# Four changes of order in a four-layer graph kernel: x loads, a batch norm, LSTM sums and differences, start-up

## The chip, the cores and the metric

One core of a Trainium2 chip runs the whole program. The metric is the device time of one execution in microseconds (us); lower is better. Everything is fp32.

## The reference

The input is x with the shape (128, 64, 256): 128 graphs of 64 nodes with 256 features, and one 64 x 64 adjacency `adj`. Four layers follow one another, each as `x = x + layer(relu(layernorm(x)), adj)`:

```python
# layer 0: two graph convolutions, then four LSTMs over windows of the nodes
h = relu(einsum('ts,bsh->bth', adj, h @ Wg0 + bg0))
h = relu(einsum('ts,bsh->bth', adj, h @ Wg1 + bg1))
for p in range(1, 5):                      # window length p
    wins = h[:, :nw*p].reshape(B*nw, p, H)
    h[:, last node of each window] = lstm_last(Wih[p-1], Whh[p-1], ..., wins)
# layer 1: masked attention, 4 heads
q, k, v = split(h @ W);  out = softmax(q k^T / 8 + mask(adj)) v
# layer 2: x @ W1^T -> batch norm -> relu -> @ W2^T -> batch norm, on A_hat h
# layer 3: three graph convolutions with adj*adj, widths 512, 1024, 256
```

The two batch norms of layer 2 take mean and variance over all 8192 tokens, so nothing of layer 3 can start before the last token of layer 2.

## The kernel before, in words

The 8192 tokens are cut into 16 blocks of 512 (`NG = 16`; a block holds 8 graphs as a tile of 128 partitions x 4 x 256). Each layer runs over the blocks. x of a block is read from HBM into a tile `xs[g]` that stays on the chip to the end. Many matrix products are done as seven products of half-size blocks instead of eight (`seven`, `sevens`); these need a few sums of one operand's blocks (`sums`, lines 206 to 209) and differences of the other's (`differences`, lines 198 to 202), four element-wise instructions each.

The order of the work on each engine is fixed when the program is built. A planner walks through the instructions as the code issues them and places each on its engine when, by its own estimate, its inputs and its buffer are ready; an instruction that comes later in the code can so be put ahead of one that comes earlier. `tc.issue_after(i)` orders the instructions of its block behind instruction `i` on the same engine, and adds no other wait. `tc.keep_in_program_order` is used for the batch norm's instructions (`normalize`). Engines run what they are given in that order. The queues that matter here are those of TensorE (PE), VectorE (DVE), ScalarE (ACT), GpSimd (POOL), and SyncE (SP), which issues nearly all transfers.

The places that the change touches:

- **Start-up.** `keep_busy(n)` (line 308) issues n matmuls on a tile of ones that do nothing but keep TensorE at work. `by_batch` (line 297) turns the two halves of `arow`, the adjacency, into `pt`; fillers stand ahead of and between the halves. `adj2` is the copy of `pt` (line 314). `ln_scale` computes a layer norm's factors: statistics on DVE (lines 92 to 95), a power on POOL (line 96), and `nmr` on DVE (line 98). Its argument `between` gives an instruction behind which `nmr` is ordered. `ln_apply` (line 111) then makes h on ACT, and `mix` (line 144) multiplies it by the adjacency on PE. rb0 is a bias row, scaled in line 424.
- **Layer 0, convolutions.** A loop over blocks runs `first_mix(g)`, `second_weights(g - 2)`, `second_mix`, `first_weights`. On DVE each iteration has the statistics, copies out of PSUM (lines 157 and 409; `copied_of[g]` is that of line 409), and the bias additions of lines 453 and 474; POOL applies the relu of line 454; PE runs the matmuls of lines 144, 445 and 469.
- **LSTM.** `first_blocks` makes the sums of the weights of an LSTM's first step. For the first LSTM all four are ordered behind `middle_copied`, the copy of iteration 8. `first_steps` makes the differences of the windows; those of the first pair of units stand in a buffer of the pool `keep` and have no order given. The tiles of `lw` ("w", five buffers) hold the weights and these sums, taken in order; `load_w` (line 275) fills them.
- **Layer 1, attention.** In iteration g, `values` makes v in two parts k = 0 and 1 (PE line 810), copies it to the single buffer `vt` (ACT line 815) and moves it with four SP transfers (line 818) into `v`. Between the parts, `load_x` (line 58) asks for the x of block g + 5, and `queries_keys` (line 788) makes q and k. `features` (lines 265 and 198 to 202) makes hT and its differences for the next iteration. Then come `scores` (line 834), `softmax` (lines 852 to 854), `turn` (PE line 870, ACT line 873) and `attend` (line 883). `to_residual` (lines 245 to 256) adds layer 0's result to x of block g + 3.
- **Layer 3.** `bring(n, ahead)` carries out n returns of layer 2's result to x (`turn_back`, PE line 1116; `add_back`, DVE line 1124) and asks for `ahead` batch norms (`normalize`: ACT line 1104, DVE line 1106). In iteration 0, blocks 0 to 7 are brought before `second_weights` (PE line 1243, ACT lines 216 and 219); after it, `bring(0, 1)` normalizes block 8 and `bring(1, 1)` returns it and normalizes block 9. `third_weights` is PE line 1288, `first_weights` line 1207.

## Time and profile before

| | |
|---|---|
| median of 3 runs | 2482.23 us (2481.2 to 2482.25) |
| profiled execution | 2480.78 us, its span 2479.0 us |
| mean granted TensorE clock | 0.999 |
| idle of PE, by the waits: the longest single ones | 2.9 us (L1116), 2.3 us (L810), 1.1 us (L870) |
| DVE, ACT, POOL busy | 61%, 46%, 18% |
| transfers | 48.00 MB, 19 GB/s in the mean |
| x loads, 512 KB each | 27, median 6.1 us from issue to landing |
| v writes, 64 KB each | 128, median 2.1 us |

A line of a timeline reads: start (us from the span's start), time from start to end, engine, line of the kernel, operation, what it writes <- what it reads, shape, and how many instructions are merged; in brackets the idle time of the engine just before, and what ended it. SPq is SyncE's queue of transfers; its time is that of issuing. L1243 is line 1243. "LDWEIGHTS" and "MATMUL" come in pairs, and an fp32 matmul shows as two records.

### The profile page before, as it was taken

The numbers are of one execution on the slowest core, as the hardware profiler recorded it, in microseconds if no ns is written. First come the engines' busy times: TensorE is split into PE (matmuls) and PEld (weight loads), VectorE is DVE, ScalarE is ACT, GpSimd is POOL, SyncE is SP. The second block draws the span as 40 slices with busy tenths as digits, with TensorE's granted clock in tenths as the row PEclk, the third lists the DMA queues.
The fourth block names the chain that finished last, engine by engine and source line by source line (L and its number), as shares of the span: only waits on it lengthen the run. The fifth ranks groups of instructions, "written<-read, shape, count | busy, mean of one in ns | idle before, by whom it ended". The sixth has DMA issues, their size and how long they took to land.

```text
span 2479.0 us, 46321 instructions
## 1 busy us (share of the span) xinstructions
PE 2454.4 (99%) x19650; PEld 2073.3 (84%) x19650; DVE 1513.1 (61%) x2705; ACT 1145.5 (46%) x2032; POOL 439.6 (18%) x368
## 2 busy tenths in 40 slices
PE   9999999999999999999999999999999999999999
PEld 6678888889999998888888864447898898888888
DVE  6758866666566565566599986325556455454544
ACT  4557745444344443444456566744333323333332
POOL 4332211111111111111133331012011111101110
PEclk9999999999999999999999999999999999999999
DMA  3200000000000000000311110010000000000000
GB/s 115 104 2 1 1 18 1 1 1 34 1 1 1 1 1 1 1 13 1 115 40 36 40 32 2 1 59 1 10 10 18 10 10 13 16 10 10 18 10 18
DMA packets 48558, 48.00 MB, mean 19 GB/s; under 512 B 3680, under 2 KB 44768, under 8 KB 48352
## 3 DMA queue, kind: packets, MB, share of 16 engines
q1 hardware_dynamic: 47360, 44.23, 5.8%
q8 instruction: 154, 2.52, 0.4%
q10 hardware_dynamic: 992, 0.82, 0.1%
q14 instruction: 52, 0.43, 0.1%
HBM read 28.26 MB, written 8.39 MB: 15 GB/s over the span
## 4 chain that ended last, share of the span: by engine, by line
PE 84%; DVE 7%; ACT 2%; POOL 1%; issue 1%; DMA 0%; SPq 0%; DVEq 0%; POOLq 0%; ACTq 0%
PE ps L526 41%; PE ps L1243 16%; PE ps L1288 8%; PE ps L1076 4%; PE ps L755 4%; PE ps L144 3%; PE ps L1207 3%; PE ps L788 1%; PE ps L469 1%; PE ps L445 1%; ACT arena L219 1%; PE ps L810 1%; DVE st L92 1%; DVE e L853 1%; DVE mx L852 1%
## 5 line engine op out<-in xcount | busy, mean ns | idle before, releaser
L526 PE MATMUL ps<-diff,s 128*128 128x256 f32 (+1 forms) x1824 | 393.5, 371 | 0.9 <-DVE diff L643 0.9
L1243 PE MATMUL ps<-arena 128*128 128x256 f32 x1792 | 392.4, 380 | 0.0
L1243 PEld LDWEIGHTS ps<-arena 128*128 128x128 f32 x1792 | 337.9, 190 | 53.9 <-issue 9.2
L526 PEld LDWEIGHTS ps<-diff,s 128*128 128x128 f32 x1824 | 345.9, 190 | 33.8 <-issue 1.6
L540 ACT ACTIVATE gates<-gates,lbias 128x512 f32<-128x512 f32 (+5 forms) x426 | 244.2, 621 | 203.4 <-DVE gates L185 147.3
L180 POOL TENSOR_TENSOR gates<-p 128x512 f32<-128x512 f32 (+1 forms) x115 | 149.3, 1298 | 879.0 <-DVE p L177 828.1
L526 PE MATMUL ps<-h,w 128*128 128x256 f32 (+1 forms) x1028 | 241.0, 371 | 0.0
L526 PE MATMUL ps<-diff,w 128*128 128x256 f32 (+1 forms) x1040 | 238.7, 370 | 0.0
L526 PEld LDWEIGHTS ps<-diff,w 128*128 128x128 f32 x1040 | 197.4, 190 | 18.2
L526 PEld LDWEIGHTS ps<-h,w 128*128 128x128 f32 x1028 | 194.7, 190 | 19.0 <-issue 0.5
L540 ACT ACTIVATE gates<-ps,lbias 128x256 f32<-128x256 f32 (+3 forms) x213 | 91.6, 476 | 247.1 <-PE ps L526 246.9
L219 ACT ACTIVATE arena<-arena 128x512 f32<-128x512 f32 (+1 forms) x160 | 88.7, 582 | 193.1 <-POOL arena L180 101.2
L180 POOL TENSOR_TENSOR arena<-arena 128x512 f32<-128x512 f32 x64 | 73.2, 1144 | 532.3 <-DVE arena L177 532.3
L1288 PE MATMUL ps<-arena 128*128 128x128 f32 x1280 | 149.9, 276 | 0.0
L185 DVE TENSOR_TENSOR gates<-p,ps 128x512 f32<-128x512 f32 (+1 forms) x115 | 76.3, 664 | 120.0 <-PE ps L526 119.8
L1288 PEld LDWEIGHTS ps<-arena 128*128 128x128 f32 x1280 | 145.7, 192 | 1.1
L96 POOL TENSOR_TENSOR rstd<-rstd,mhalf 128x4 f32<-128x4 f32 (+1 forms) x66 | 66.1, 1002 | 423.0 <-DVE rstd L95 411.6
L185 DVE TENSOR_TENSOR arena<-arena,ps 128x512 f32<-128x512 f32 x64 | 39.7, 621 | 152.9 <-PE ps L1243 87.4
L526 PE MATMUL ps<-state,w 128*128 128x256 f32 (+1 forms) x512 | 116.1, 370 | 0.9 <-ACT p L173 0.8
L176 DVE TENSOR_TENSOR p<-p,ps 128x512 f32<-128x512 f32 (+1 forms) x131 | 86.6, 661 | 48.5 <-PE ps L526 48.4
L526 PE MATMUL ps<-state,s 128*128 128x256 f32 (+1 forms) x512 | 115.8, 369 | 0.0
L189 DVE TENSOR_TENSOR gates<-p,ps 128x512 f32<-128x512 f32 (+1 forms) x115 | 76.6, 666 | 63.9 <-PE ps L526 63.2
(206 smaller groups left out, 4070.2 us busy)
## 6 DMA issues: line engine op xcount, KB each, us to landing
x<-in_x SPq DMA_DIRECT2D x27, 512.0 KB, 6.1
v<-vt SPq DMA_DIRECT2D x128, 64.0 KB, 2.1
out<-x SPq DMA_DIRECT2D x15, 512.0 KB, 3.0
w<-in_wih SPq DMA_DIRECT2D x4, 1024.0 KB, 6.1
w<-in_whh SPq DMA_DIRECT2D x3, 1024.0 KB, 5.0
arena<-in_l3w SPq DMA_DIRECT2D x3, 1024.0 KB, 5.3
w<-in_wqkv SPq DMA_DIRECT2D x1, 768.0 KB, 4.5
x<-in_x SPq DMA_DIRECT2D x2, 256.0 KB, 3.0
```

What stands on the lines that cost most here:

```text
L144: last = nc.tensor.matmul(pss[b][half * 64 : half * 64 + 64, c, t, :], lhsT=src[rows, t, col : col + 64], rhs=a2[rows, :], start=True, sto ...
L176: nc.vector.tensor_tensor(p1, p1, ps[2], ALU.add)
L180: nc.gpsimd.tensor_tensor(out=out[1][1], in0=p1, in1=p5, op=ALU.add)
L185: nc.vector.tensor_tensor(out[0][1], p1, ps[1], ALU.add)
L189: last = nc.vector.tensor_tensor(to, p, q, ALU.add)
L219: nc.scalar.activation(o, o, func)
L526: nc.tensor.matmul(ps[:, r], lhsT=wc[:, j, :], rhs=bc, start=first and r == 0 and c == 0, stop=True, skip_group_check=True,)
L540: nc.scalar.activation(o, ps, func, bias=lbias[:, col : col + 1])
L755: nc.tensor.matmul(ps, lhsT=w1[:, c, m * P : (m + 1) * P], rhs=a[:, 2 + c, :], start=(c == 0), stop=(c == 1),)
L1076: nc.tensor.matmul(pss[m], lhsT=w2[c // 2][:, c % 2, m * P : (m + 1) * P], rhs=a[:, c, :], start=(c == 0), stop=(c == 3),)
L1243: nc.tensor.matmul(ps[:, r, :], lhsT=w[:, c, col : col + P], rhs=b[:, c, :], start=first and r == 0 and c == 0, stop=c == 1, skip_group_ch ...
L1288: nc.tensor.matmul(ps[:, t, :], lhsT=w[:, c, t * P : (t + 1) * P], rhs=b[:, c, :], start=first and t == 0 and c == 0, stop=c == 3, skip_gr ...
```

## The change

- Start-up: 6 fillers instead of 7 ahead of the first half of `pt`, 2 instead of 3 between the halves, 2 behind; the copy of `adj2` is placed ahead of the second half's `nmr` instead of the first's.
- LSTM: the four sums of the first LSTM's weights come one each behind `copied_of[5]` to `copied_of[8]`; the four differences of its first pair come one each behind `copied_of[10]` to `copied_of[13]`. They are written as loops over the four operations, with an order for each.
- Attention: `load_x` of block g + 5 is ordered behind the last of the four transfers of `values(..., (0,))`.
- Layer 3: in iteration 0, `bring(0, 1)` stands ahead of `second_weights` instead of behind it.

```diff
+    def each_behind(behind, i):
+        return tc.issue_after(behind[i].ins) if behind else nullcontext()
...
+    def differences(eng, b11, b12, b21, b22, t1, t2, t3, t4, negate=False, behind=None):
         t4a, t4b = (b21, t2) if negate else (t2, b21)
-        return eng.tensor_tensor(out=t4, in0=t4a, in1=t4b, op=ALU.subtract).ins
...
+        ops = ((t1, b12, b11), (t3, b22, b12), (t2, b22, t1), (t4, t4a, t4b))
+        for i, (t, p, q) in enumerate(ops):
+            with each_behind(behind, i):
+                last = eng.tensor_tensor(out=t, in0=p, in1=q, op=ALU.subtract)
+        return last.ins
...
-            keep_busy(7)
+            keep_busy(6)
             pt = bank((P, NODES))
-            by_batch(pt, arow, lambda b, last: keep_busy(3 - b, last))
+            by_batch(pt, arow, lambda b, last: keep_busy(2, last))
             lns = [
-                ln_scale(xs[0][:, 0:2], lambda: nc.vector.tensor_copy(adj2, pt), 2),
-                ln_scale(xs[0][:, 2:4], None, 2),
+                ln_scale(xs[0][:, 0:2], None, 2),
+                ln_scale(xs[0][:, 2:4], lambda: nc.vector.tensor_copy(adj2, pt), 2),
             ]
...
-                    differences(nc.vector, *x[0], *x[1], *ts, negate=True)
+                    differences(
+                        nc.vector, *x[0], *x[1], *ts, negate=True,
+                        behind=copied_of[10:14] if pool is keep else None,
+                    )
...
-            with tc.issue_after(middle_copied):
-                w0 = first_blocks(w_next[0], lw.tile([P, 2, 1024], F32, tag="w", name="s"))
+            w0 = first_blocks(
+                w_next[0], lw.tile([P, 2, 1024], F32, tag="w", name="s"), copied_of[5:9]
+            )
...
-            values(hT_all, v, (0,))
+            moved = values(hT_all, v, (0,))
             if g + NK + 1 < NG:
-                load_x(xs[g + NK + 1], g + NK + 1)
+                with tc.issue_after(moved):
+                    load_x(xs[g + NK + 1], g + NK + 1)
...
                 brought = ready
+                bring(0, 1)
...
                     for b, pss in later:
                         add_back(b, pss)
-                bring(0, 1)
             bring(1, 1)
```

`sums` is rewritten in the same way as `differences`, `first_blocks` hands `behind` on to it, and `values` returns its last transfer.

## The prediction

> **What bounds the kernel now.** I read the head of the page first: TensorE (PE) has almost no room.

> ```profile
> PE 2454.4 (99%) x19650; PEld 2073.3 (84%) x19650; DVE 1513.1 (61%) x2705; ACT 1145.5 (46%) x2032; POOL 439.6 (18%) x368
> ```

> With a span of 2479.0 us, PE is idle for 24.6 us in all. The change removes no matmul but two start-up fillers, so its gain can only come from that idle time, and each part has to be laid on a named gap. So the second view is the waits of PE (us in total, times, longest):

> ```profile
> PE ps L1116 <- ACT arena L1104: 3.2, 2, 2.9
> PE ps L810 <- ACT hT L265: 2.3, 1, 2.3
> PE ps L144 <- POOL h L454: 1.8, 4, 0.8
> PE ps L870 <- ACT e L854: 1.1, 1, 1.1
> ```

> The timeline puts the first at 1739.50 (layer 3), the second at 1239.81 and the fourth at 1246.37 (attention), and 1.2 of the third at 103.12 and 104.57 (layer 0). Third, the busy time by stretches of 3.4 us around 1739.5 (columns: length, busy PE, PEld, DVE, ACT, POOL, then the granted clock):

> ```profile
> 1736.60:1740.00 3.40, 0.50 (x5) 0.50 (x6) 3.40 (x4) 1.89 (x3) 0.00 (x0) 1.00 0.00 0
> 1740.00:1743.40 3.40, 3.40 (x72) 2.95 (x71) 3.25 (x6) 0.49 (x2) 0.00 (x0) 0.50 0.00 0
> ```

> The reader is to see that the gap is paid twice: PE idles, and then runs one stretch at half clock, busy but slow. From the first L1116 to the first L1288 takes 3.40 there and 2.06 one iteration later (1790.00 to 1792.06), and the next 48 L1288 take 5.84 against 5.62: 1.56 us more.

> [...]

> **Part E, the batch norm ahead of second weights.** bring(0, 1) issues two instructions for block 8: ACT L1104 (0.75) and DVE L1106 (0.54). No transfer goes with them. Now they come after second_weights in the code. ACT's timeline around it (start, duration, idle before it):

> ```profile
> 1710.16 0.58 ACT L154 COPY arena<-ps 128x512 f32<-128x512 f32 x1 [0.35 <-PE ps L144]
> 1714.20 0.58 ACT L173 COPY arena<-ps 128x512 f32<-128x512 f32 x1 [3.46 <-PE ps L1243]
> ...
> 1738.11 0.63 ACT L219 ACTIVATE arena<-arena 128x512 f32<-128x512 f32 x1 [1.89 <-DVE arena L189]
> 1738.64 1.50 ACT L1104 ACTIVATE arena<-arena,n2sh,n2sc 128x512 f32<-128x512 f32 x2
> ```

> L1104 stands behind the last L219 on ACT's queue, and PE's transposes L1116 at 1739.50 wait for it, though its data was ready long before. Moved, it falls in the idle 3.46 before 1714.20. That cover is 2.7 more than it needs; without it 0.75 would fall on the path. DVE's half moves from idle time at 1717.46 to just before the last differences, which PE's third product reads: L200 ends at 1714.42, with 0.54 more at 1714.96; the 112 L1243 are 14 products in 24.34, 1.74 each, so the third starts at 1712.22 + 3.48 = 1715.70. Hidden with 0.7 to spare. Then PE goes from L1243 into L1116 as at 1790.00, where no gap is. Late next could be the sums of third weights; L206 ends at 1737.47 and the second product would start near 1742.0. Gain: 2.94 of gap. The 1.56 of half clock goes too, but [...] not every run before needs to have paid it: I take half, 0.8 (0 to 1.56). **E: 3.7** (2.0 to 4.5).

> **Part D, loads of x.** In the timelines of SP and ACT:

> ```profile
> 1227.38 2.29 SPq L58 DMA_DIRECT2D x<-in_x  x4
> 1230.09 2.69 SPq L818 DMA_DIRECT2D v<-vt  x4
> ```

> ```profile
> 1238.68 0.58 ACT L815 COPY vt<-ps 128x512 f32<-128x512 f32 x1 [2.47 <-DMA v<-vt]
> 1239.16 1.08 ACT L265 COPY hT<-ps 128x512 f32<-128x512 f32 x2
> ```

> All twelve x loads (512 KB each) are issued between 1211.5 and 1232.8, because nothing holds them. The four writes of v behind them land near 1238.6, some 6 us after the last is issued, where the median is 2.1. vt has one buffer, so its next copy on ACT waits; hT, queued behind that, holds PE's L810 for 2.27; and because DVE's L198, scores and softmax follow hT, L870 at 1246.37 waits 1.05, where ordinary iterations lose 0.13. Moved, eleven loads (x5 to x15) each go behind the fourth v write of their iteration. Then v lands by 1232.8 + 2.1 = 1234.9; ACT ends L245 at 1236.2, L815 runs at once, and hT starts at 1236.7 instead of 1239.16. L810 can start when L834 ends (1237.53): the 2.27 goes. From hT's start to L870 takes 7.21 now (1239.16 to 1246.37), so L870 comes at 1243.9 instead of 1246.37. Gain 2.5; 3.2 if hT also gets as early as later on. The added wait: SP holds a load until the v writes are out. Behind it stand only the next writes of v, issued 6.4 us later; x of block g+5 is first added in iteration g+2, over 25 us on. **D: 2.5** (2.0 to 3.2).

> **Parts B and C, sums and differences of the LSTM.** DVE's timeline in layer 0:

> ```profile
> 91.28 0.69 DVE L206 TENSOR_TENSOR w<-w 128x512 f32<-128x512 f32 x1 [2.24 <-DMA w<-in_wih]
> ...
> 98.02 0.69 DVE L199 TENSOR_TENSOR diff<-h 128x512 f32<-128x512 f32 x1 [0.73 <-ACT h L477]
> ...
> 100.44 0.68 DVE L453 TENSOR_TENSOR h<-ps,rb 128x512 f32<-128x512 f32 x1
> ```

> In a quiet iteration L453 starts 2.03 after PE's L445; here the L445 began at 94.06, so it is over 4 us late, and POOL's L454 and PE's L144 follow it: gaps of 0.43 and 0.76, and 0.12 at 98.99. Between stand four differences (2.7), four sums for the second LSTM (2.7) and waits of 2.24 and 0.73. The change spreads the differences over iterations 10 to 13 and the first LSTM's sums over 5 to 8, one of 0.68 each. DVE idles 1.90 + 1.03 + 0.41 + 0.22 = 3.6 per quiet iteration of 9.47 (around 77 us), so each is hidden; without that cover, 0.68 each. What moves along: three weight loads of 1 MB start at 85.19, 0.7 after the first sum at 84.51, in the same pool; with that sum in iteration 5 they should start near 57. Then the second LSTM's sums and their DMA wait come in iterations 6 and 7, without the differences: 2.24 + 2.7 + 1.4 is less than two iterations' slack. The x loads behind them on SP are used 25 us later. I take 1.1 of the 1.31 (0.3 to 1.3). **B and C: 1.1.**

> **Part A, start-up.** From the timeline:

> ```profile
> 6.19 0.32 PE L297 MATMUL ps<-ident,arow 64*64 64x64 f32 x2
> 6.55 0.22 DVE L314 COPY adj<-ps 128x64 f32<-128x64 f32 x1 [0.86 <-PE ps L297]
> 6.69 0.22 DVE L98 SCALAR_TENSOR_TENSOR nmr<-mv,rstd 128x2 f32<-128x2 f32 x2
> 6.88 1.58 ACT L111 ACTIVATE h<-x,nmr,rstd 128x256 f32<-128x256 f32 x3 [1.94 <-DVE nmr L98]
> ```

> The first nmr is ordered behind the copy of adj, which waits for L297, and L297 for fillers. Now one filler matmul fewer runs ahead of each half (7 took 3.35, so 0.48 each) and the copy stands ahead of the second nmr only. The second half of arow lands at 1.31 + 4.3 = 5.6, so L297 runs near 5.7; the first rstd is done at 5.81, nmr at 5.9, L111 at 6.05 instead of 6.88: 0.83. rb0, from the same queue, could arrive late at L424 and take part of it; fewer fillers could also leave TensorE at half clock longer. I take 0.7 (-0.5 to 0.85).

> **Sum.** The profiled execution is 2480.78, 1.78 beside its span and 1.45 under the median of 2482.23. For it: 0.7 + 1.1 + 2.5 + 4.5 = 8.8, so 2472.0. For the median, with half the clock cost: 8.0, so **2474.2**. About 0.2% (5.0 us) is what a measurement of this kernel can tell from no change.

> **Rivals.** *Gaps that change their releaser*: for it speaks that ACT does L873 and L245 before L815, and that L870 and the second LSTM's sums keep their waits: D 0.5, B and C 0.3, A 0.2, E 2.9 without clock cost: 3.9, giving 2478.3, no change. Against it: the later iterations, where the same chains run with 0.13 or nothing. Chance 0.16. That the planner puts the norm or the loads elsewhere than the code asks belongs here. *Loads that collide in each iteration*: slower. ACT's L815 already waits 3.1 for v (at 1258.02), and L174 behind it ends 0.1 before the exp that PE waits for; so when a load of x delays the second four writes of v, nearly all of it reaches PE, 11 times. The point is a landing over 6.4 us after issue. On a calm queue x lands in 3.7 to 4.7 (97 to 115 us), in the burst up to 8.7. At 1.4 us over: 15.4 lost, D's 2.5 not gained, 5.5 gained elsewhere: +9.9, 2492.1. Chance 0.06, since one load at a time is the calm case. The forecast: 0.78.

> **Range.** All upper ends give 9.85 (2472.4), all lower ones 3.8 (2478.4); with part of the first rival 2472.0 to 2479.0.

> **What would show it.** Right: no L1116 gap near 1730 and no 0.50 clock after it; no L810 gap near 1235 and L870 at 0.1 to 0.9; one x load per attention iteration landing within 5 us; no L454 gaps; first L111 near 6.1. Wrong: L815 waiting over 3.5 in every iteration, or new L144 gaps near 70.

## The result, and the profile after

The changed kernel takes **2474.7 us** at the median of 8 runs (2473.82 to 2476.59), the kernel before on the same chip 2481.72 (8 runs, 2479.93 to 2483.10): a ratio of 0.9973, 95% interval 0.9962 to 0.9984, or 7.0 us less. A second comparison on one chip gave 2474.54 against 2481.88, 0.9972 (0.9961 to 0.9983). The forecast was 2474.2. The profiled execution of after took 2476.59, the longest of its eight; its span is 2474.8.

From the page of after: the head of the first part, and two rows of the DMA issues (KB each, median us to landing).

```profile
PE 2454.1 (99%) x19646; PEld 2073.2 (84%) x19646; DVE 1512.6 (61%) x2705; ACT 1145.7 (46%) x2032; POOL 439.8 (18%) x368
...
x<-in_x SPq DMA_DIRECT2D x27, 512.0 KB, 4.1
...
w<-in_wih SPq DMA_DIRECT2D x4, 1024.0 KB, 7.5
```

This execution is only 4.2 us shorter than the profiled one of before. PE's busy time is that of before within 0.3 us, and idle time went from 24.6 us to 20.7. That the busy time is equal is chance: a stretch of 3.41 us at half clock went in layer 3, and full clock came at 13.6 us instead of 6.0 (both below). In a second profile of the change, with a span of 2472.7, PE is busy for 2451.4 and idle for 21.3. The waits of PE in after (us in total, times, longest) show which ones changed:

```profile
PE ps L882 <- ACT e L866: 2.2, 4, 1.3
PE ps L452 <- DVE m L417: 2.0, 3, 0.9
...
PE ps L144 <- POOL h L461: 0.4, 1, 0.4
...
PE ps L1129 <- ACT arena L1117: 0.3, 1, 0.3
```

Three of the four waits that the prediction shows have fallen: L1116 (now L1129) from 3.2 to 0.3, L810 (L821) from 2.3 to no row at all, L144 behind the POOL from 1.8 to 0.4. The fourth, L870 (now L882), has grown from 1.1 to 2.2, and L452 has 2.0 where L445, its line of before, had 1.2 in two rows. These two are the losses that the prediction lacks. After has 1.8 at L846 as well, for which the profile names no releaser; before has 0.6 there, and the fourteen profiles of this document spread from nothing to 1.8 whatever the change, so it is not counted.

**The norm.** The timeline of ScalarE, then the busy time by stretches at layer 3 (columns as in the prediction: length, PE, PEld, DVE, ACT, POOL, clock), both of after:

```profile
1710.60 0.59 ACT L154 COPY arena<-ps 128x512 f32<-128x512 f32 x1 [0.35 <-PE ps L144]
1711.08 0.82 ACT L1117 ACTIVATE arena<-arena,n2sh,n2sc 128x512 f32<-128x512 f32 x1
1714.64 0.58 ACT L173 COPY arena<-ps 128x512 f32<-128x512 f32 x1 [2.75 <-PE ps L1256]
```

```profile
1736.60:1740.00 3.40, 3.40 (x83) 3.07 (x82) 3.31 (x5) 1.51 (x4) 0.00 (x0) 1.00 0.00 0
1740.00:1743.40 3.40, 3.40 (x33) 3.40 (x32) 3.40 (x5) 0.61 (x2) 0.00 (x0) 1.00 0.00 0
```

L1117 sits in the idle stretch where the prediction laid it: the 3.46 ahead of L173 became 2.75. PE is busy through both stretches, at full clock in both, where before it had 0.50 busy in the first and half clock in the second. VectorE's half fell ahead of the last differences, as foreseen (1713.39, 0.54 long), and PE did not wait for it.

**The loads.** SyncE's and ScalarE's timelines of after at the start of the attention:

```profile
1217.52 2.64 SPq L829 DMA_DIRECT2D v<-vt  x4
1220.21 0.59 SPq L58 DMA_DIRECT2D x<-in_x  x1
1222.42 8.69 SPq L829 DMA_DIRECT2D v<-vt  x8
1231.15 0.59 SPq L58 DMA_DIRECT2D x<-in_x  x1
```

```profile
1227.96 0.58 ACT L826 COPY vt<-ps 128x512 f32<-128x512 f32 x1 [4.59 <-PE ps L799]
1228.44 0.59 ACT L173 COPY p<-ps 128x512 f32<-128x512 f32 x1
1228.92 0.60 ACT L174 COPY p<-ps 128x512 f32<-128x512 f32 x1
1229.54 1.28 ACT L866 ACT_TABLE_LOAD   x1
1230.83 1.06 ACT L866 ACTIVATE e<-e 128x1024 f32<-128x1024 f32 x1
```

From here on one load of x goes behind the first v writes of each iteration, and the 27 loads land in a median of 4.1 us, where before has 6.1. The wait of hT is gone. But L826, the copy of the values for iteration 1, has ScalarE idle for 4.59 ahead of it. The releaser named there, PE, had long been done. Of the four writes that still read vt, the last one whose landing is on record, the third, landed at 1227.53; in the second profile of the change the fourth landed at 1226.17 and the copy began at 1226.41. Behind L826 on the same queue stand the copies L173 and L174 that the products need and the exponentials that L882 needs: PE waits 0.37 at 1229.09 and 1.30 at 1231.94.

```profile
1231.94 1.09 PE L882 MATMUL ps<-ident,e 128*128 128x128 f32 x8 [1.30 <-ACT e L866]
```

**The LSTM's weights.** VectorE's timeline of after:

```profile
60.67 0.69 DVE L460 TENSOR_TENSOR h<-ps,rb 128x512 f32<-128x512 f32 x1 [1.04 <-PE ps L452]
64.78 1.29 DVE L216 TENSOR_TENSOR w<-w 128x512 f32<-128x512 f32 x2 [3.41 <-DMA w<-in_wih]
65.99 0.68 DVE L157 COPY m<-ps 128x512 f32<-128x512 f32 x1
66.59 0.68 DVE L417 COPY m<-ps 128x512 f32<-128x512 f32 x1
```

The weights of the second LSTM are now asked for at 57.27 and land at 64.75. Their first two sums stand on VectorE's queue ahead of the copies of a block, wait 3.41 and take 1.29. PE waits 0.87 at 67.32 for the copy behind them, and 0.36 at 72.50:

```profile
67.32 3.72 PE L452 MATMUL ps<-wg,m 128*128 128x256 f32 x16 [0.87 <-DVE m L417]
```

The gaps near 104 are gone.

### The profile page after: what moved, and what is told of

It reads as the page before. It is cut to its first block, busy times and chain, and to the rows that moved or that the text cites. A ratio compares the mean times of both kernels' runs of the same rounds, so it can differ in the third digit from the quotient of the medians.

```text
span 2474.8 us, 46316 instructions
## 1 busy us (share of the span) xinstructions
PE 2454.1 (99%) x19646; PEld 2073.2 (84%) x19646; DVE 1512.6 (61%) x2705; ACT 1145.7 (46%) x2032; POOL 439.8 (18%) x368
## 4 chain that ended last, share of the span: by engine, by line
PE 89%; DVE 6%; ACT 2%; issue 1%; POOL 1%; DMA 0%; SPq 0%; ACTq 0%; DVEq 0%; POOLq 0%
PE ps L533 41%; PE ps L1256 16%; PE ps L1301 8%; PE ps L1089 4%; PE ps L766 4%; PE ps L144 4%; PE ps L1220 3%; PE ps L476 2%; PE ps L452 2%; PE ps L799 2%; PE ps L821 1%; ACT arena L227 1%; POOL arena L180 1%; PE ps L882 1%; DVE st L92 0%
## 5 line engine op out<-in xcount | busy, mean ns | idle before, releaser
L189 DVE TENSOR_TENSOR gates<-p,ps 128x512 f32<-128x512 f32 (+1 forms) x115 | 76.7, 667 | 63.9 <-PE ps L533 63.2
```

What stands on the lines that cost most here:

```text
L189: last = nc.vector.tensor_tensor(to, p, q, ALU.add)
```

## The experiments

Each run is timed against the kernel before on the same chip; the intervals are those of the ratio, and 0.0004 of it is 1 us. Four kernels do one part of the change each.

**The norm alone.**

```
                 brought = ready
+                bring(0, 1)
...
-                bring(0, 1)
```

> The kernel before with only the batch norm of block 8 asked for ahead of second weights. Theory: this part carries most of the 7 us, because it takes away a PE gap of 2.9 us and, where the idle window fell on it, a stretch at half clock worth 1.56 more: 2.9 to 4.5 us faster, no L1116 gap in layer 3 over 0.3, no clock of 0.5 inside layer 3. Rival (the four parts share the gain about evenly): 2 us or less.

Measured: 2477.67 against 2482.15, 0.9980 (0.9973 to 0.9987): 4.5 us less, the upper end of what was expected, in an interval of 3.2 to 6.7. Its profile has no wait at the transposes of block 8 and no half clock near 1740. It has one at 1240.68 instead, behind the gap of 2.45 at L810, which this run leaves alone.

**The loads alone.**

```
-                load_x(xs[g + NK + 1], g + NK + 1)
+                with tc.issue_after(moved):
+                    load_x(xs[g + NK + 1], g + NK + 1)
```

> The kernel before with only the loads of x behind the first v writes of their iteration. Theory from the profile after: the gap of 2.27 at L810 goes and the 1.05 at L870 goes, but x of block 5 now lies right ahead of iteration 0's second v writes, which land 5.5 us after issue instead of 2.1 and bring back about 1.7 us of PE waits in iteration 1 (L788 on ACT, L870 on ACT): 1 to 2 us faster. Rival, the prediction's own sum: 2.5 us faster (2.0 to 3.2) with no PE gap over 0.9 in iteration 1.

Measured: 2479.70, 0.9990 (0.9982 to 0.9998): 2.45 us less. That is the prediction's 2.5, but the interval, 0.5 to 4.5 us, holds the expected 1 to 2 as well. The profile shows a gain less a loss, as expected: no L810 gap, and 1.30 at the transposes of iteration 1.

**The LSTM's sums and differences alone.**

```
-            with tc.issue_after(middle_copied):
-                w0 = first_blocks(w_next[0], ...)
+            w0 = first_blocks(w_next[0], ..., copied_of[5:9])
...
+                        behind=copied_of[10:14] if pool is keep else None,
```

> The kernel before with only the LSTM's sums and differences spread over layer 0. Theory from the profile after: the PE gaps near 99 to 105 us (1.31) go, but the second LSTM's weights are asked for 28 us earlier, its first sum waits 3.4 us on DVE for them around 64, and new PE gaps of about 0.87 and 0.36 come near 67 and 72: 0 to 0.3 us faster. Rival, the prediction's own sum: 1.1 us faster.

Measured: 2480.81, 0.9994 (0.9986 to 1.0002): 1.3 us less, not told from nothing by the time alone. The profile carries it: from the first mix to the first LSTM matmul it takes 155.90 us (6.93 to 162.83) against 157.09 before (7.53 to 164.62), and 156.9 to 157.7 in the five other profiles with start-up and layer 0 as before. Of the two expected waits only the second came, 0.36 at 70.32: the weights landed 6.7 us after they were asked for, VectorE waited 2.63 for them and not 3.41, and PE lost nothing at L452.

**The start-up alone.**

```
-            keep_busy(7)
+            keep_busy(6)
...
-                ln_scale(xs[0][:, 0:2], lambda: nc.vector.tensor_copy(adj2, pt), 2),
-                ln_scale(xs[0][:, 2:4], None, 2),
+                ln_scale(xs[0][:, 0:2], None, 2),
+                ln_scale(xs[0][:, 2:4], lambda: nc.vector.tensor_copy(adj2, pt), 2),
```

> The kernel before with only the start-up changed (fillers 6, 2, 2 and the copy of adj2 ahead of the second nmr). Theory: the first L111 starts 0.8 us earlier, but what reaches the end is 0.7 when TensorE is at full clock by about 7 us and nothing or a loss of up to 1 when it comes later[...]: 0 to 0.7 us faster in the median. Rival, the prediction's own: 0.7.

Measured: 2481.36, 0.9998 (0.9990 to 1.0006): 0.8 less, which the interval does not tell from nothing. By its clock record, TensorE came to full clock only at 13.9 us, as in after (13.6); the kernel before had it at 6.0. That raised a suspicion against the fewer fillers. So the copy was moved and the fillers left:

```
             keep_busy(7)
...
+                ln_scale(xs[0][:, 0:2], None, 2),
+                ln_scale(xs[0][:, 2:4], lambda: nc.vector.tensor_copy(adj2, pt), 2),
```

> The kernel before with one part of the start-up edit: the copy of the adjacency behind the second half's scale, the fillers left at 7, 3 and 2 (12 as before, where the whole edit has 10). Theory: the fewer fillers leave PE short of work in a window of the start in executions where adj lands late, so that the full clock comes at 13.6 us instead of 5 to 6 and eats up the gain; with the fillers left, the full clock comes by 7 us, the first mix starts 0.3 us earlier, and the gain is 0.3 to 0.5 us. Rival: the clock's start has nothing to do with the fillers: full clock past 13 us is seen here too in a profile whose window has the same phase, or the gain is nought or the 0.8 of the whole edit. The time alone will hardly tell 0.4 from 0.8; the clock and the gap ahead of the first mix in the profile do.

Measured: 2482.25 against 2481.98, 1.0001 (0.9993 to 1.0009), so no gain is shown. Full clock came at 4.1 us. By itself that fits the theory of the fillers; the last runs below overturn it.

**The clock.** Nine, then six, extra matmuls in the gap ahead of the transposes of block 8, in the kernel before:

```
+            if g == 8 and k == 0:
+                for _ in range(9):   # 6 in the second
+                    nc.tensor.matmul(ps[0][:, 0, :], lhsT=ident, rhs=o3[:, 0:256], ...)
             turn_back(g, ps, ks=[k])
```

> The kernel before, with nine matmuls of 128x256 on data that is ready (their result is overwritten) put on PE right ahead of the transposes of block 8, into the bank that these transposes write. They take nine times 0.216, some 1.9 us, and lie inside the gap of 2.94 us ahead of L1116; the transposes still wait for the norm. My theory of the clock: an almost idle stretch of 2.94 us lets the clock fall to a half for one window of 3.41 us; with the gap cut to about 1 us the clock stays full after 1739 and the kernel gains up to 1.56 us in the executions whose window fell into the gap, that is 0.5 to 1.6 us at the median, while the chain to the transposes doesn't move. Rival: the half clock has nothing to do with the gap (or costs nothing on the path): then the time doesn't change, within 0.3 us, or the half clock near 1740 is seen again. If the gain is 0.5 to 1.6, then the edit E, worth 4.5 alone, is the gap of 2.94 and this; if it is nought, E's excess over 2.94 is a second effect of the earlier norm.

Measured: 2483.67 against 2481.98, 1.0004 (0.9996 to 1.0012). The expectation priced a matmul at one record of 0.216; each is two, so nine took 3.89 us and put the transposes off. From them to the next transposes it took 20.71 instead of 22.27, though, and no half clock came. So again with six:

> The kernel before with six extra matmuls in the place where clock_fill had nine: each took 0.432 us (two passes of 0.216), so nine took 3.89 us, 0.78 more than the gap, and put the transposes of block 8 off by 0.78. Six take 2.59 us and fit into the gap of 2.94. Theory: from the transposes of block 5 to those of block 8 it takes 36.9 us as before, from there to the next 20.7 instead of 22.3, no half clock near 1740, and the time is 0.5 to 1.6 us less than before. Rival: no change of time within 0.3 us, since most executions do not fall to the half clock in that gap.

The timeline of PE and the stretches in this run:

```profile
1739.94 2.75 PE L1132 MATMUL ps<-arena,ident 128*128 128x256 f32 x12
1742.53 1.04 PE L1116 MATMUL ps<-ident,arena 128*128 128x128 f32 x8
```

```profile
1739.60:1743.00 3.40, 3.40 (x20) 2.99 (x19) 2.92 (x4) 3.04 (x5) 0.00 (x0) 1.00 0.00 0
1743.00:1746.40 3.40, 3.40 (x86) 3.17 (x85) 3.40 (x6) 0.58 (x1) 0.00 (x0) 1.00 0.02 5
```

PE does 2.6 us of useless work here, the norm is still late, and the clock stays full: the transposes take the 1.04 of after and the next ones come 20.7 later (1742.53 to 1763.25). VectorE's order shifted a little as well (the transposes came 36.41 after those that started at 1706.12, where before has 36.92 for the same pair). The time, 2480.69 against 2481.88, 0.9995 (0.9987 to 1.0004), is 1.2 less, in the expected place but not told from nothing.

The two profiles do not show that the fillers kept the clock up. A boundary of the clock's windows (last section) falls into the gap in both. An estimate from that boundary and the start of the fillers: left idle, the gap would have been 1.38 and 1.56 us on its two sides in the first run and 1.65 and 0.78 in the second, and in no profile did a window with up to 1.74 us of idle time drop the clock. What the half clock costs is shown by the seven profiles that keep the gap of 2.94. From these transposes to the next, the five that fell to half clock have 22.2 to 22.3 us, and the two that did not have 20.76 and 20.77. The seven with the gap filled or gone have 20.7. So the half clock costs some 1.5 us, in an execution that has it.

**What the transposes wait for.** First the loads behind the second writes of v:

```
-            if g + NK + 1 < NG:
-                load_x(xs[g + NK + 1], g + NK + 1)
...
+            moved = values(hT_all, v, (1,))
+            if g + NK + 1 < NG:
+                with tc.issue_after(moved):
+                    load_x(xs[g + NK + 1], g + NK + 1)
```

> The kernel before with the x loads ordered behind the second writes of v instead of the first (the write on record in the change is the first). In the loads edit alone the first x load lay right ahead of the second writes of v in iteration 1 and the probabilities' transposes waited 1.30 us for them, beside 0.37 at the products. Theory: with the load behind the second writes both gaps go, the L810 gap of 2.27 stays away, and the gain over before is 3.0 to 4.2 us, 1 to 1.7 more than the loads edit's 2.45. Rival: the loads then meet the first writes of the next iteration, or the gap at the transposes has another cause: the gain is 2.5 or less.

Measured: 2479.82, 0.9991 (0.9983 to 0.9999), 2.2 less. No load lies between any more, and PE still waits at the transposes. ScalarE's timeline in this run:

```profile
1226.67 0.59 ACT L815 COPY vt<-ps 128x512 f32<-128x512 f32 x1 [3.73 <-PE ps L788]
1227.15 0.59 ACT L173 COPY p<-ps 128x512 f32<-128x512 f32 x1
```

The theory that the load ahead of the writes makes the wait fell: counted from the first matmul of the values, the copy comes at 15.5 us here, at 16.3 in after and at 15.5 in a second profile of the change, and 1.09 of the wait stays at the transposes. The same queue in the kernel before:

```profile
1223.61 0.59 ACT L815 COPY vt<-ps 128x512 f32<-128x512 f32 x1 [1.10 <-DMA v<-vt]
1225.82 0.59 ACT L173 COPY p<-ps 128x512 f32<-128x512 f32 x1 [1.62 <-PE ps L788]
...
1228.54 1.06 ACT L854 ACTIVATE e<-e 128x1024 f32<-128x1024 f32 x1
1229.50 0.57 ACT L815 COPY vt<-ps 128x512 f32<-128x512 f32 x1
```

There the next copy to vt stands behind the exponentials. With the loads moved, the order on ScalarE's queue is another: that copy stands ahead of L173, and it needs the one vt. So a second vt, in the changed kernel (`rsrow`, a tile of the start-up, moves to the set-up pool to make room):

```
-                vt = ap_.tile([P, 2, D], F32, tag="vt", name="vt", bufs=1)
+                vt = ap_.tile([P, 2, D], F32, tag="vt", name="vt", bufs=2)
```

> The changed kernel with a second buffer for vt, the tile that takes the values from PSUM before they are written to v (and rsrow kept in the set-up pool, to make room). In the profile of the change ScalarE's copy L826 stands ahead of the copies L173 in iteration 1 and waits for the second writes of v in iteration 0 to land, since they read the one vt; the products then wait 0.37 us and the transposes L882 1.30 us. With the loads behind the second writes (no load between) 1.09 of it stayed, so my theory is that the order on ScalarE and the one buffer make the wait and not the load ahead. Expected: L826 waits for no DMA, the gap at L882 near 1231 falls below 0.3, and the kernel is 0.9 to 1.6 us faster than the changed kernel in the same call (ratio to before about 0.9968 to 0.9964 if the change has 0.9973). Rival: the transposes wait for something else (the table load ahead of the exponentials, VectorE): the gap stays at 1 us or more and the time is the change's.

Measured: 2473.41 (2472.64 to 2475.36) against 2474.54 of the change on the same chip, 1.1 us less, though with 5 and 7 runs that overlap; to before 0.9969 (0.9956 to 0.9981). ScalarE in this run, and PE:

```profile
1224.52 0.59 ACT L826 COPY vt<-ps 128x512 f32<-128x512 f32 x1 [1.47 <-issue]
1225.39 0.59 ACT L172 COPY p<-ps 128x512 f32<-128x512 f32 x1 [0.28 <-PE ps L799]
```

```profile
1228.60 0.60 PE L799 MATMUL ps<-hT,wsum 128*128 128x256 f32 x2
1229.21 1.09 PE L882 MATMUL ps<-ident,e 128*128 128x128 f32 x8
```

L882 starts at 1229.21 with no idle time ahead. In the change's second profile it stood there thus:

```profile
1230.39 1.09 PE L882 MATMUL ps<-ident,e 128*128 128x128 f32 x8 [1.16 <-ACT e L866]
```

The wait was the order and the one buffer. The table load of 1.28 ahead of the exponentials, which the expectation names as a rival, still stands on ScalarE's queue (1226.81), and PE does not wait. Part of the wait comes back one iteration later, where the change has 0 and 0.25 in its two profiles:

```profile
1243.23 1.09 PE L882 MATMUL ps<-ident,e 128*128 128x128 f32 x8 [0.75 <-ACT e L866]
```

From the first matmul of the values to the transposes of iteration 3 it takes 47.08 us here and 48.33 and 47.78 in the change, so 0.7 to 1.3 is gained.

**The sums of the second LSTM later**, the LSTM edits otherwise as in the change:

```
-                            w0 = first_blocks(w_next[0], weight_tile())
+                            w0 = first_blocks(w_next[0], weight_tile(),
+                                [copied_of[i] for i in (9, 11, 13, 14)] if p == 1 else None)
```

> The kernel before with the LSTM edits alone, but the sums of the second step's weights ordered one each behind the copies of blocks 9, 11, 13 and 14 of layer 0. In the LSTM edits alone those sums stood near 64 us on VectorE, and it waited there for the weights' load (3.41 us in the profile of the change). Theory: the wait at 64 goes, with the PE gaps of 0.3 to 0.9 behind it, and none comes near 99 to 105: the gain over before is 1.3 to 2.0 us. Rival: the gaps at 67 to 72 cost nothing in the executions that are timed, or the four sums set new gaps near 90 to 110: the gain is that of the LSTM edits alone, 1.3 us, or less.

Measured: 2480.28 against 2481.98, 0.9991 (0.9983 to 0.9999): 1.7 less, which the time alone does not tell from the 1.3 of the LSTM edits. VectorE where the change waited:

```profile
59.13 0.69 DVE L460 TENSOR_TENSOR h<-ps,rb 128x512 f32<-128x512 f32 x1 [1.03 <-PE ps L452]
60.23 0.69 DVE L157 COPY m<-ps 128x512 f32<-128x512 f32 x1 [0.41 <-PE ps L144]
60.84 0.68 DVE L417 COPY m<-ps 128x512 f32<-128x512 f32 x1
```

The copies go 0.41 after their matmuls; PE has no gap over 0.25 us from 18 to 530. First mix to first LSTM matmul: 155.28 us (6.81 to 162.09), 0.62 less than the LSTM edits alone.

**All three mends**, the second vt, the late sums, and 12 fillers with the copy moved:

> The changed kernel with three mends: two buffers for vt, the sums of the second step's weights behind the copies of blocks 9, 11, 13 and 14, and 12 fillers at the start as in the kernel before (the copy of the adjacency stays behind the second half's scale). If the gaps found in the profile of the change (0.87 and 0.36 near 67 to 72, 0.37 and 1.30 near 1229 to 1232, and up to 2 us of half clock at the start) are real in every execution, 2 to 4 us less than the change: 2470.5 to 2472.5 where the change is at 2474.7. Rival: only those of the attention are, or the mends shift other waits: 0 to 1.6 us less.

Measured: **2472.63** (2471.53 to 2473.70), 0.9963 (0.9949 to 0.9976) to before, the fastest of all: 9.3 us less than before and 1.9 less than the change, whose runs on the same chip all lie above its highest. That lies between the rival's 1.6 and the lower end of the expected 2 to 4; the wait of 0.74 at the transposes of iteration 2 is here too. The change again, on the same chip:

> The changed kernel as it is, beside the kernel before and the three others of this call on one chip. Theory: the ratio of the first comparison, 0.9973 within 0.0010, 6 to 8 us less than before; its four parts alone came to 4.5, 2.45, 1.3 and 0.8, 9.05 together, so if they add up it should be 9 us less. In its profile: if the full clock at the start again comes past 10 us, ten fillers are too few for a start like this in more than a chance window (the profiles with twelve had it at 4.1 to 6.0, both with ten at 13.6 and 13.9); if it comes by 7 us, the late clock was a matter of the window's phase.

Measured: 2474.54 (2473.98 to 2475.39), 0.9972 (0.9961 to 0.9983), 7.3 less. The four parts alone came to 9.05; each carries an interval of some 2 us to either side, so by the times the difference proves no interaction. The profiles show where parts do not add: the first LSTM matmul comes at 162.83 with the LSTM edits alone, but at 165.00 and 164.22 in the change. Six profiles with start-up and layer 0 as before have it at 164.5 to 165.1.

These last runs also answer the question of the fillers. The change, run again with its ten, had full clock at 4.9 us, and the run with two vt, also with ten, at 4.3; the one with all three mends, with twelve, had it at 13.9. The theory that ten fillers are too few falls: late and early starts of the clock come with either number.

## Why the prediction was right, step by step

**E, the norm: 3.7 predicted, 4.5 measured alone.** The mechanism holds line by line: hidden on ScalarE, hidden on VectorE, no successor to the wait. The profiles give its size more closely than the times. From the transposes that start at 1702.58 in before to those of block 9 (1761.77), before and the four others that fell to half clock have 59.1 to 59.25 us, the two with the gap and full clock 57.69, and all five with the norm moved 54.5. So the part is worth 3.15 or 4.65, and 4.2 in the mean of these seven. The term that was too small is the half clock, taken at one half of 1.56; that half was the author's estimate. It came in five of the seven (before, the loads alone in both placings, the start-up alone, the copy alone) and not in two (the LSTM edits alone, and with late sums). At 5 in 7 the prediction's sum is 4.05. The boundaries of the clock's windows lay elsewhere in each of three executions, the first at 2.59 us of the span in before, at 3.39 in after and at 1.47 in the second profile of the change; how they cut the gap of 2.94 in two runs, one with half clock and one without, is in the last section.

**D, the loads: 2.5 predicted, 2.45 measured alone.** The sum is right and its working is not; that the two agree is luck. The gap at L810 is not 2.27 in every execution: the eight profiles with the loads as before have 1.8 to 4.2, 2.8 in the mean, and five of them fell to half clock behind it, which the prediction did not count. From the first matmul of the values to the transposes of iteration 3 these eight take 49.3 to 53.4 us, 50.9 in the mean, and the four with the loads moved and one vt 47.8 to 48.3. The failed step is "L870 comes at 1243.9 instead of 1246.37", which leaves the order on ScalarE as it was. With the loads alone it comes at 1244.43: the waits of 2.27 and 1.05 both went, but moving the loads also moved the copy to vt ahead of L173 in iteration 1, and 1.30 came there. The two errors had opposite signs. The rival of collisions in each iteration did not come: one iteration pays, and a load behind the second writes didn't save it.

**B and C, the LSTM: 1.1 predicted, 1.3 measured alone.** The gaps near 104 went, by spreading as worked out, and the weights were asked for at 57.27 where the prediction has 57. The failed step is "2.24 + 2.7 + 1.4 is less than two iterations' slack". The slack is there, but not ahead of the copies L157 and L417, which stand behind the waiting sums on VectorE; the load took 7.5 us to land and VectorE waited 3.41, not 2.24. In the change 0.87 and 0.36 were given back, in its second profile 1.27 and 0.35, which is all that the gaps near 104 had cost; the run with the late sums has neither. The prediction named new L144 gaps near 70 as a sign that it would be wrong. Gaps near 70 came, at L452 and L476, and in this point it was.

**A, the start: 0.7 predicted, 0.8 alone, within its error of nothing.** What can be read is where it lands: the first nmr at 5.79 and L111 at 5.99 for 6.05. VectorE's and ScalarE's timelines of after:

```profile
5.79 0.16 DVE L98 SCALAR_TENSOR_TENSOR nmr<-mv,rstd 128x2 f32<-128x2 f32 x1
6.11 0.22 DVE L323 COPY adj<-ps 128x64 f32<-128x64 f32 x1 [0.16 <-PE ps L305]
```

```profile
5.99 1.58 ACT L111 ACTIVATE h<-x,nmr,rstd 128x256 f32<-128x256 f32 x3 [1.11 <-DVE nmr L98]
```

The first mix comes at 7.15 in after and at 6.75 in its second profile, where before has 7.53. The full 0.83 does not reach PE: at half clock the fillers themselves hold PE until 7.15, and in other executions adj is late (PE waited 0.4 to 1.1 us for it ahead of the second half in four of the fourteen profiles). Between two executions of the changed kernel, one with full clock at 13.6 and one at 4.9, the first LSTM matmul differs by 0.78 us (165.00 and 164.22), as much as the whole part was to bring; the first L452, which runs in that stretch, takes 5.47 us at half clock in after and 3.69 in before (there L445).

**The sum.** 8.0 was predicted for the median, 7.0 and 7.3 were measured, and the sum fits better than its terms. By the profiles E and D brought more than theirs, 4.2 and some 2.9 for 3.7 and 2.5. A with B and C, 1.8 together in the prediction, brought next to nothing in the change: its first LSTM matmul comes at 164.22 to 165.00, before's at 164.62. That these errors came out so near the forecast is luck. The two new waits cost some 1.9, by the run with all mends; what it leaves of them is the 0.74 of iteration 2. The rival in which the gaps only change their releaser was right in kind at two places and wrong in size.

## What to carry to other kernels

A gap of TensorE of 2.94 us, where a window of its clock has 3.41, cost the gap and, in five of seven profiles, some 1.5 us more; price both, and weigh the second by how often so much of the gap falls into one window. When an instruction is given a new place, read every engine's queue again, for the order of what was not named in the edit can change with it, and a copy into a single buffer that slips ahead of the chain is enough (1.30 us of PE here). Work that is spread into idle time can bring its loads forward with it (the weights here, from 85.19 us to 57.27): what counted in VectorE's wait of 3.41 was not the idle time of a whole iteration but what stood directly behind the waiting instruction. And a part that gains alone need not gain beside the others (the first LSTM matmul at 162.83 us with the LSTM edits alone, at 165.00 and 164.22 in the change): follow one point of the program, such as the first matmul of a layer, through the profiles of all runs.

## What the runs showed of the hardware

```profile
1738.10:1741.51 3.41, 1.46 (x36) 1.30 (x40) 3.41 (x5) 2.04 (x3) 0.00 (x0) 1.00 0.00 0
1741.51:1744.92 3.41, 3.41 (x61) 3.29 (x51) 3.31 (x6) 0.59 (x1) 0.00 (x0) 0.50 0.00 0
```

The LSTM edits alone:

```profile
1738.71:1742.12 3.41, 1.67 (x51) 1.51 (x55) 3.41 (x5) 2.04 (x3) 0.00 (x0) 1.00 0.00 0
1742.12:1745.54 3.42, 3.42 (x62) 3.35 (x55) 3.32 (x7) 0.96 (x2) 0.00 (x0) 1.00 0.02 5
```

With 1.46 busy the next window runs at half clock, with 1.67 at full. Idle time of up to 1.74 us in a window cost itself alone here. From this an estimate for the gap of 2.94: if the boundaries fall anywhere with equal chance, a window holds enough of the gap in 72 to 84% of the executions (a limit of 1.95 or of 1.74), near the 5 in 7 that the profiles have.

**When the clock comes up.** In eleven profiles it was full at 4.1 to 6.0 us, in three at 13.6 to 13.9, with ten fillers and with twelve. The last four filler records take 1.22 us in after, at 6.00, and 0.71 in before, at 6.44, where the clock is full. In the late ones a boundary fell at 3.4 to 3.7 us, and the window behind it was followed by another at half clock although PE idled 0 to 0.44 us in it; so was the next, with 0.63 to 0.89 idle. Why stays open; the small transposes of adj lie in it, and no run separated them.

**Landing times vary.** The same 1 MB load of the second LSTM's weights landed 6.4 to 7.9 us after issue in the six profiles that ask for it near 57, and 5.9 to 6.1 in the eight that ask for it near 85; the same gap at L810 was 1.8 to 4.2 us. One profile gives such a term one sample.
